# The first gate row of an FFN: by SBUF-to-SBUF transfers instead of by way of memory

## The chip, the cores and the metric

The kernel runs on one core of a Trainium2 chip. The metric is the device time of one execution in microseconds (us): the median of three runs. Engines are named as in the profile: PE (matmuls; PEld is its weight load), DVE (the vector engine), ACT (activations), POOL (GpSimd), and SP, whose queue (SPq) issues most transfers.

## What is computed

Two layers act on `x`, 32 batches of 128 tokens with 128 features, all in float32. Each layer adds an FFN of a conditioned mixture of experts to `x`:

```
x = x + L0_ffn(L0_cond(x, cond))
x = x + L1_ffn(L1_cond(x, cond))
```

The change lies in `L0_ffn`. It takes c = L0_cond(x), runs all 8 experts on every token and weights them with gates from two softmaxes:

```
router_probs = softmax(c @ w_router);  gate_weights = softmax(c @ w_gating / 0.1)
h = silu(c @ w_gate[e]) * (c @ w_up[e])          # for each expert e
expert_out[e] = h @ w_down[e]
cw = router_probs * gate_weights;  cw = cw / (sum(cw) + 1e-9)
out = sum over e of cw[e] * expert_out[e]
```

The kernel puts the gate on the input of the up projection: it multiplies c by row e of `cw` before `w_up[e]`, which is the same since silu sees only the other projection.

## The kernel before

Activations lie with features on the 128 partitions and tokens along the free axis. The 4096 tokens are cut into 8 blocks of 512 (`NB`, `TB`; 4 batches each), and a superblock is 4 blocks (`SB`). The result c of the first mixture is `c0T[blk]`, the slices of the tile `c0all`.

**Before the FFN.** Units of the first mixture run in a software pipeline, `up` of the next unit ahead of `down` of the present one. The last three are the shared expert's blocks 5, 6 and 7: `shared_up` (L297, matmuls on L302) and `shared_down` (L309, matmuls on L313); L315 on DVE adds the result into `c0T[blk]`. A table of hooks, `between` (L687), hangs the FFN's gates for blocks 0 to 3 into these last units: the router's logits, `ffn_logits(0)`, `ffn_gates(0)` (an Exp on ACT on L657, then a chain of small DVE instructions on L658 to L665 that ends in the tile `cwT`), and at the start of `shared_down(6)` `first_rows` (L683).

**The way of a gate row.** `first_rows` calls `gates_to_dram("f", 0)` (L626): a PE transpose of `cwT` (L630), a DVE copy to the SBUF tile `t`, named `fg_sb` (L632), and a 64 KB transfer to a tile in memory, `fg` (L634, SP). After the transpose, partition 16 e + b of `t` holds the gates of expert e for the 128 tokens of batch b. Then `fetch_rows(0)` (L670) issues four transfers on SP (L676), each of which brings the rows of experts k and k + 4 of one block to partition 32 k of an SBUF tile named `fgT`. One row is 512 gates, those of an expert for a block.

**The FFN.** Its 64 units are (block, expert), block by block. For each, `gate_ahead` (L747) has POOL spread a row over 128 partitions (`spread`, L707; the broadcast is L710) into one of four `bc` buffers, tile `fg`; `input_ahead` (L754) has DVE multiply it with `c0T[blk]` (L759) into the tile `cg`. `ffn_up` (L762) starts with `gate_ahead(i + 2)` and `input_ahead(i + 1)`, then takes four chunks of 128 hidden features: a gate projection from `c0T` and `wg_t`, an up projection from `cg` and `wu_t` (both L262, in column halves of 64), and `glu` (L713): Silu on ACT (L715) and a product on DVE (L716) into `hf`. `ffn_down` (L787) runs the down projection (L798) with DVE combinations of `hf` and `t` (L777 to L780). The calls for the first unit stand in this order: `gate_ahead(0)`, `gate_ahead(1)`, `input_ahead(0)`, then `ffn_up(0, 0)`.

**What orders the work.** Projections take PSUM banks from a ring of six (`mm_tile`, L118), in the order of the source; a bank is used again when ACT (gate projection) or DVE (up projection) has read it. Each engine works through its own list in order. The lists are drawn up when the kernel is built, and a matmul need not stand where the source has it unless `keep_in_program_order` pins it; L262 with halves of 64 columns is not pinned. SP issues in order too, and a transfer that waits holds up those behind it. Among them are loads for the second layer (L901), which wait for weights tiles to come free.

Of the kernel before, what the change touches and what calls it, by code (L numbers as in the profile page):

```python
# [32 lines left out]
F32 = mybir.dt.float32  # L33
# [5 lines left out]
P = 128  # L39
B, S, D = 32, 128, 128  # L40
BB = 4
TB = BB * S
# [56 lines left out]
def adaln_ffn(  # L99
# [3 lines left out]
    nc = tc.nc  # L103
# [5 lines left out]
    work = ctx.enter_context(tc.tile_pool(name="work", bufs=2))  # L109
# [8 lines left out]
    def mm_tile(name):  # L118
        taken["mm"] += 1
        return banks[:, (taken["mm"] - 1) % NM, :]  # L120
# [505 lines left out]
    def gates_to_dram(kind, sb):  # L626

        gates, name = held.pop((kind, sb)), f"{kind}g{sb}"
        ps = mm_tile(f"{name}_ps")
        nc.tensor.transpose(ps[:, :P], gates.rearrange("p e b -> p (e b)"), ident)  # L630
        t = work.tile([P, P], F32, tag="gsb", name=f"{name}_sb", bufs=1)
        V.tensor_copy(t, ps[:, :P])  # L632
        d = dram.tile([P, P], F32, tag=name, name=name)
        nc.sync.dma_start(out=d, in_=t)  # L634
        in_dram[kind, sb] = d.rearrange("(e b) t -> e (b t)", e=E1)
# [45 lines left out]
    held, in_dram, fgates = {}, {}, {}  # L681

    def first_rows():  # L683
        gates_to_dram("f", 0)
        fgates[0] = fetch_rows(0)
# [21 lines left out]
    def spread(row, name):  # L707

        bc = work.tile([P, TB], F32, tag="bc", name=name, bufs=4)
        nc.gpsimd.partition_broadcast(bc, row)  # L710
        return bc
# [33 lines left out]
    gated, bcast, sums_of = {}, {}, {}  # L745

    def gate_ahead(i):  # L747

        if i < len(ffn_units):
            blk, e = ffn_units[i]  # L750
            g, k = divmod(e, 4)
            bcast[i] = spread(fgates[blk][32 * k : 32 * k + 1, g, :], f"fg_{blk}_{e}")

    def input_ahead(i):  # L754

# [6 lines left out]
    def ffn_up(blk, e):  # L762
        i = blk * EF + e
        gate_ahead(i + 2)
        input_ahead(i + 1)
        h = work.tile([P, NC, TB], F32, tag="h", name=f"hf_{blk}_{e}", bufs=3)
        cg = gated.pop((blk, e))
        for c in range(NC):
            cs = slice(c * P, (c + 1) * P)
            g, u = mm_tile(f"g_{blk}_{e}_{c}"), mm_tile(f"u_{blk}_{e}_{c}")  # L770
            by_columns(g, wg_t[:, e, cs], c0T[blk], D // 2)
            by_columns(u, wu_t[:, e, cs], cg, D // 2)
            glu(g, u, h[:, c, :], f"sf_{blk}_{e}_{c}")
        b11, b12, b21, b22 = (h[:, k, n] for k in (slice(0, 2), slice(2, 4)) for n in (slice(0, HALF), slice(HALF, TB)))
        t = work.tile([P, 3, 2, HALF], F32, tag="bsum", name=f"t_{blk}_{e}", bufs=2)
        t2, t3, t4 = (t[:, j] for j in range(3))
        V.tensor_tensor(t3, b22, b12, ALU.subtract)  # L777
        V.tensor_tensor(b12, b12, b11, ALU.subtract)  # L778
        V.tensor_tensor(t2, b22, b12, ALU.subtract)
        V.tensor_tensor(t4, t2, b21, ALU.subtract)  # L780
        if blk == 0:
            a_prepare(e)
        if rest:
            rest.pop(0)()
        return b11, b12, b21, b22, t2, t3, t4
# [68 lines left out]
    def after_ffn(blk, e):  # L854

        if (blk, e) == (0, 2):
            logits_ahead("lg", par[:, AT["wr"]], c0T, 1)
        if (blk, e) == (0, 3):
            ffn_logits(1)
            ffn_gates(1)  # L860
        if (blk, e) == (0, 5):
            gates_to_dram("f", 1)
        if e == 4 and blk + 1 < NB:
            fgates[blk + 1] = fetch_rows(blk + 1)
        if (blk, e) == (SB, 3):
            logits_ahead("l1", par[:, AT["r1x"]], xT, 0)
        if (blk, e) == (SB, 4):
            l1_scores(0)
        if (blk, e) == (SB, 6):
            route(0)  # L870
        if (blk, e) == (SB + 1, 0):
            gates_to_dram("r", 0)
# [30 lines left out]
    x1T = xT  # L903

    gate_ahead(0)
    gate_ahead(1)
    input_ahead(0)

# [172 lines left out]
    def strip(group, j):  # L1081

        first, n, size = GROUPS[group]
        b, half = divmod(j, SB // n)
        return first + b, slice(half * size, (half + 1) * size)
# [120 lines left out]
    for j in (2, 3):  # L1206
        b, at = strip(2, j)
# [12 lines left out]
    for j, ps in enumerate(outs):  # L1220
        b, at = strip(2, j)
        t = fins[j // 2][:, at]
# [4 lines left out]
    for j in (0, 2, 1, 3):  # L1227
        b, at = strip(2, j)
# [81 lines left out]
```

## Time and profile before

| what | value |
|---|---|
| median of three runs | 964.26 us (963.98 to 965.26) |
| the profiled execution, its own time | 964.74 us |
| its span, first to last instruction | 963.0 us |
| instructions | 15674 |
| mean granted TensorE clock | 0.999 |
| PE busy | 953.2 us, 99% of the span |
| DVE busy | 594.8 us, 62% |
| ACT busy | 352.0 us, 37% |
| POOL busy | 74.9 us, 8% |
| matmuls on L262 for gate and up projections | 263.1 and 262.8 us, 1024 instructions each |
| broadcasts of gate rows, L710 on POOL | 64, mean 1142 ns |

The span is the time from the first to the last instruction of one profiled execution; its own time is 1.74 us longer. The busy times are sums over the whole span, so an engine can be busy 99% of it and still stand still for some hundred nanoseconds at one place. Waits are inferred from semaphore events, and one that ends on several of them is put down to the one that came last. In the lists of instructions in order of time, the columns are start and duration in us, engine, line, operation, what is written and read, and the number of instructions merged into the row; in brackets stands the idle time before it.

### The profile page before, as it was taken

The page shows a single profiled execution, that of the slowest core. Times are in us where ns is not written, and L with a number is a line of the kernel's source. Part 1 is how long each engine was busy: PE and PEld are TensorE (multiplying, and loading weights), DVE is VectorE, ACT ScalarE, POOL GpSimd, SP SyncE. Part 2 cuts the span into 40 slices and gives each one's busy share as a digit, 9 for nine tenths or more (in the row PEclk, how much of TensorE's full clock was granted, in tenths as well). Part 3 has the DMA queues.
Part 4 walks back from the last instruction along what each step waited for, and adds up shares of the span by engine and source line. Part 5 has one row for each costly group of instructions (what it writes and reads, how often), then busy time and mean ns, then how long its engine had stood idle before and what let it go on. Part 6 is the DMA issues. An engine that isn't in the chain of part 4 may idle for free.

```text
span 963.0 us, 15674 instructions
## 1 busy us (share of the span) xinstructions
PE 953.2 (99%) x6132; PEld 444.3 (46%) x6132; DVE 594.8 (62%) x1121; ACT 352.0 (37%) x622; POOL 74.9 (8%) x86
## 2 busy tenths in 40 slices
PE   9999999999999999999999999999999999999997
PEld 4588983444444444444444444444444443322333
DVE  4444565766866776686676786667667655633423
ACT  5354544232322322232231332223223223557674
POOL 0000002101101010110101011010110000000000
PEclk9999999999999999999999999999999999999999
DMA  9655641000000000000000000000000004040101
GB/s 331 229 156 167 209 134 49 1 1 4 1 1 2 1 1 1 1 1 1 2 2 1 1 2 3 1 2 1 1 1 1 1 1 89 2 91 1 45 1 45
DMA packets 22850, 38.13 MB, mean 40 GB/s; under 512 B 1968, under 2 KB 13232, under 8 KB 22768
## 3 DMA queue, kind: packets, MB, share of 16 engines
q1 hardware_dynamic: 22192, 36.48, 12.5%
q8 instruction: 53, 0.87, 0.4%
q10 hardware_dynamic: 576, 0.54, 0.2%
q14 instruction: 29, 0.24, 0.1%
HBM read 34.65 MB, written 2.36 MB: 38 GB/s over the span
## 4 chain that ended last, share of the span: by engine, by line
PE 83%; DVE 1%; ACT 1%; issue 0%; POOL 0%; DVEq 0%; POOLq 0%; ACTq 0%
PE banks L262 57%; PE banks L798 20%; PE banks L938 3%; PE banks L1032 1%; PE banks L313 1%; ACT hl L1040 0%; PE banks L601 0%; PE banks L302 0%; PE banks L616 0%; PE banks L546 0%; ACT L657 0%; DVE cg L759 0%; PE banks L630 0%; DVE pg L1026 0%; DVE pT L1027 0%
## 5 line engine op out<-in xcount | busy, mean ns | idle before, releaser
L715 ACT ACTIVATE sf<-banks 128x512 f32<-128x512 f32 x256 | 152.7, 597 | 433.8 <-PE banks L262 423.3
L716 DVE TENSOR_TENSOR hf<-sf,banks 128x512 f32<-128x512 f32 x256 | 175.1, 686 | 181.6 <-PE banks L262 180.5
L262 PE MATMUL banks<-c0all,wg_t 128*64 128x512 f32 x1024 | 263.1, 593 | 0.0
L262 PE MATMUL banks<-cg,wu_t 128*64 128x512 f32 x1024 | 262.8, 592 | 0.3 <-DVE cg L759 0.3
L262 PEld LDWEIGHTS banks<-cg,wu_t 128*64 128x64 f32 x1024 | 73.3, 137 | 146.9 <-issue 126.3
L262 PEld LDWEIGHTS banks<-c0all,wg_t 128*64 128x64 f32 x1024 | 72.8, 137 | 121.4 <-issue 108.8
L710 POOL PARTITION_BROADCAST fg<-fgT x64 | 72.5, 1142 | 652.7 <-DVE cg L759 492.0
L798 PE MATMUL banks<-t,wd_t 128*64 128x256 f32 x512 | 121.0, 379 | 0.0
L798 PE MATMUL banks<-hf,wd_t 128*64 128x256 f32 x512 | 104.2, 379 | 0.0
L798 PEld LDWEIGHTS banks<-hf,wd_t 128*64 128x64 f32 x512 | 53.3, 137 | 55.4 <-issue 36.8
L798 PEld LDWEIGHTS banks<-t,wd_t 128*64 128x64 f32 x512 | 70.1, 137 | 0.0
L536 ACT ACTIVATE h<-banks,w 128x256 f32<-128x256 f32 (+3 forms) x136 | 49.7, 434 | 49.4 <-PE banks L533 49.3
L798 PE MATMUL banks<-hf,a_sum 128*64 128x256 f32 x512 | 66.1, 379 | 0.0
L798 PE MATMUL banks<-t,a_sum 128*64 128x256 f32 x256 | 65.7, 379 | 0.0
L778 DVE TENSOR_TENSOR hf<-hf 128x512 f32<-128x512 f32 x64 | 63.0, 985 | 2.2
L262 PE MATMUL banks<-xall,rw_t 128*32 128x512 f32 x512 | 58.3, 593 | 0.2 <-ACT hl L1040 0.2
L262 PE MATMUL banks<-xall,sws 128*32 128x512 f32 x512 | 57.4, 593 | 0.2 <-ACT hl L1040 0.2
L546 PE MATMUL banks<-h,w 128*128 128x256 f32 (+3 forms) x272 | 52.6, 338 | 0.5 <-PEq L591 0.5
L533 PE MATMUL banks<-x,w 128*128 128x256 f32 (+3 forms) x272 | 52.2, 337 | 0.0
L533 PEld LDWEIGHTS banks<-x,w 128*128 128x128 f32 x272 | 45.3, 190 | 4.4 <-issue 1.0
L546 PEld LDWEIGHTS banks<-h,w 128*128 128x128 f32 x272 | 44.6, 190 | 5.4 <-DVE c0all L553 1.3
L1013 ACT ACTIVATE hr<-banks 128x512 f32<-128x512 f32 x64 | 36.9, 592 | 25.5 <-PE banks L262 25.4
(217 smaller groups left out, 778.3 us busy)
## 6 DMA issues: line engine op xcount, KB each, us to landing
w<-in_experts SPq DMA_DIRECT2D x36, 514.5 KB
wg_t<-in_w_gate SPq DMA_DIRECT2D x8, 256.0 KB
wu_t<-in_w_up SPq DMA_DIRECT2D x8, 256.0 KB
wd_t<-in_w_down SPq DMA_DIRECT2D x8, 256.0 KB
gates<-rg SPq DMA_DIRECT2D x4, 512.0 KB
gates<-rg SPq DMA_DIRECT2D x8, 256.0 KB
xall<-in_x SPq DMA_DIRECT2D x7, 256.0 KB
out<-fin SPq DMA_DIRECT2D x6, 256.0 KB
```

The costliest lines, as they stand in the source:

```text
L262: mm = nc.tensor.matmul(ps[own, :], lhsT=w[:, own], rhs=x, start=True, stop=True)
L313: nc.tensor.matmul(y, lhsT=sw2_t[:, c, :], rhs=h[:, c, :], start=(c == 0), stop=(c == NC - 1))
L533: nc.tensor.matmul(ps[c][:, :m, :n], lhsT=w1, rhs=x[:, :m, :n], start=True, stop=True)
L536: nc.scalar.activation(h[:, c, :m, :n], ps[c][:, :m, :n], AF.Gelu_apprx_tanh, bias=bias)
L546: nc.tensor.matmul(y[:, :m, :n], lhsT=w2, rhs=h[:, c, :m, :n], start=(c == 0), stop=(c == NC - 1))
L710: nc.gpsimd.partition_broadcast(bc, row)
L715: silu = nc.scalar.activation(s, ps_gate, AF.Silu)
L716: V.tensor_tensor(h, s, ps_up, ALU.mult)
L778: V.tensor_tensor(b12, b12, b11, ALU.subtract)
L798: nc.tensor.matmul(y[half, n], lhsT=w[:, c, :], rhs=h[:, c, :], start=first, stop=(e == EF - 1 and last))
L938: in_order(nc.tensor.matmul(y[32 * j : 32 * (j + 1)], lhsT=w, rhs=h, start=first, stop=last))
L1013: in_order(nc.scalar.activation(h[:, at, :], ps, AF.Gelu))
```

## The change

For the first superblock of the FFN's gates, `gates_to_dram` issues four transfers of 512 bytes each on SP before the transfer to memory. They take partitions 0 to 3 of `t`, which are expert 0's gates for the four batches of block 0, and lay them side by side on one partition of a new SBUF tile of 512 elements. `gate_ahead(0)` spreads that tile. The transfer to memory and the four of `fetch_rows(0)` stay as they are, and all other rows come from them.

```
--- before
+++ after
@@ -630,6 +630,11 @@
         nc.tensor.transpose(ps[:, :P], gates.rearrange("p e b -> p (e b)"), ident)
         t = work.tile([P, P], F32, tag="gsb", name=f"{name}_sb", bufs=1)
         V.tensor_copy(t, ps[:, :P])
+        if (kind, sb) == ("f", 0):
+
+            held["first row"] = work.tile([1, TB], F32, tag="first", name="first_row", bufs=1)
+            for b in range(BB):
+                nc.sync.dma_start(out=held["first row"][:, b * P : (b + 1) * P], in_=t[b : b + 1, :])
         d = dram.tile([P, P], F32, tag=name, name=name)
         nc.sync.dma_start(out=d, in_=t)
         in_dram[kind, sb] = d.rearrange("(e b) t -> e (b t)", e=E1)
@@ -749,7 +754,8 @@
         if i < len(ffn_units):
             blk, e = ffn_units[i]
             g, k = divmod(e, 4)
-            bcast[i] = spread(fgates[blk][32 * k : 32 * k + 1, g, :], f"fg_{blk}_{e}")
+            row = held["first row"] if i == 0 else fgates[blk][32 * k : 32 * k + 1, g, :]
+            bcast[i] = spread(row, f"fg_{blk}_{e}")
```

More of the change, by code (lines that the diff above doesn't have):

```diff
@@ L632, in gates_to_dram @@
         V.tensor_copy(t, ps[:, :P])
+        if (kind, sb) == ("f", 0):
+            held["first row"] = work.tile([1, TB], F32, tag="first", name="first_row", bufs=1)
+            for b in range(BB):
+                nc.sync.dma_start(out=held["first row"][:, b * P : (b + 1) * P], in_=t[b : b + 1, :])
         d = dram.tile([P, P], F32, tag=name, name=name)
@@ L751, in gate_ahead @@
             g, k = divmod(e, 4)
-            bcast[i] = spread(fgates[blk][32 * k : 32 * k + 1, g, :], f"fg_{blk}_{e}")
+            row = held["first row"] if i == 0 else fgates[blk][32 * k : 32 * k + 1, g, :]
+            bcast[i] = spread(row, f"fg_{blk}_{e}")
     def input_ahead(i):
```

## The prediction

> **What bounds the kernel now.** I read the page first. PE is busy 953.2 of 963.0 us at a granted clock of 0.999:
>
> ```profile
> span 963.0 us, 15674 instructions
> PE 953.2 (99%) x6132; PEld 444.3 (46%) x6132; DVE 594.8 (62%) x1121; ACT 352.0 (37%) x622; POOL 74.9 (8%) x86
> ```
>
> So the change can only win what PE stands still because of the first gate row. Next, the chain of waits around the FFN's start (start, length in us, what):
>
> ```profile
> 158.33 4.31 PE banks L313 x10
> 162.64 0.02 issue
> 162.66 0.76 DVE c0all L315
> 163.42 0.01 issue
> 163.43 0.04 POOLq L710
> 163.47 0.13 issue
> 163.60 0.81 POOL fg L710
> 164.41 0.02 issue
> 164.43 1.16 DVE cg L759
> 165.58 0.04 issue
> 165.63 11.38 PE banks L262 x52
> ```
>
> The row does sit on this chain: POOL's broadcast, DVE's product, then PE. The list of instructions in order of time on PE tells how long PE really stands:
>
> ```profile
> 162.55 2.79 PE L262 MATMUL banks<-c0all,wg_t 128*64 128x512 f32 x12
> 165.63 2.79 PE L262 MATMUL banks<-cg,wu_t 128*64 128x512 f32 x12 [0.28 <-DVE cg L759]
> 168.25 1.03 PE L262 MATMUL banks<-c0all,wg_t 128*64 128x512 f32 x4
> 169.11 1.03 PE L262 MATMUL banks<-cg,wu_t 128*64 128x512 f32 x4
> 169.97 1.03 PE L262 MATMUL banks<-c0all,wg_t 128*64 128x512 f32 x4
> ```
>
> The source has gate and up projections in turns; the built order is three gate projections, then three up projections, so PE has work that needs no gate. Groups of four (one projection) start 0.86 us apart (168.25, 169.11, 169.97), and three after a pause take 2.62 (165.63 to 168.25). Three gate projections from 162.55 therefore end their turn at 165.17. PE goes on at 165.63. **The stall is 0.46 us**, 0.05% of the kernel; the 0.28 in the row is smaller because it runs from the modelled end. Last, SP's queue and its waits:
>
> ```profile
> 158.68 0.34 SPq L634 DMA_DIRECT2D fg<-fg_sb  x1
> 161.50 2.47 SPq L676 DMA_DIRECT2D fgT<-fg  x4
> 164.08 0.39 SPq L901 DMA_DIRECT2D sws<-in_s_w  x1
> ```
>
> ```profile
> SPq L676 <- DMA fg<-fg_sb: 2.4, 1, 2.4
> ```
>
> The row goes out at 158.68, is in memory at 161.48, is read back from 161.50 and lands at 163.40 by the trace's semaphore records: 4.72 us. The chain names L315 (end 163.41) as what released POOL, 0.01 us after that landing. POOL's next two broadcasts follow the landings of their rows by the same 0.02 us, so I take the transfer as the cause.
>
> **First row.** Four transfers of 512 bytes are added. The nearest row for their issue is L676, also to one partition: starts at 161.50, 162.26, 162.86 and 163.44, so 0.75 and then 0.6 apart. The fourth goes out at 158.68 + 0.75 + 0.6 + 0.58 = 160.61. No SBUF-to-SBUF transfer is in the trace. Above, I bound the landing by the reads of L676, 1.78 to 1.93 us from issue; below, by what is known of its halves: L634, which reads SBUF, has its first packet 0.84 us after issue, and L676, which writes SBUF, lands 0.4 us after its packets: 1.25. The fourth lands at 161.9 to 162.5; I take 162.5, since L676 is the whole path. That is 0.9 us earlier than 163.40.
>
> The Trainium skill speaks against this: "DMA: Bandwidth & Descriptors", in "Rules for kernel authors", wants many small transfers merged into one, for under 64 KB nearly all is overhead, and "Anatomy of one DMA" gives a fixed cost of about 2.0 us each (fitted on the GpSimd path). Four in a row at that price land at 166.7, the first product is ready at about 168.6, and PE would stand 3 us longer than now. The rows say that the fixed parts overlap: four reads take 1.78 + 1.94 = 3.7 us in all, not 8. The rows decide.
>
> POOL now waits for four transfers instead of one; its wait instruction takes 0.04 us, so 0.13 more. Broadcast from 162.5 + 0.2 + 0.13 = 162.8 to 163.6 (0.80 each). DVE's product stands behind L315, which ends at 163.41, so it starts at 163.65. It took 1.145 us beside POOL's second broadcast, 0.68 elsewhere; it ends between 164.35 and 164.8. PE wants it at 165.17: the margin is 0.4 to 0.8 us, and **the whole 0.46 goes**. The other 0.3 to 0.8 us of the gain lie beside PE's three gate projections and are worth nothing.
>
> **What the four issues push back.** Everything behind them on SP starts 0.75 + 0.6 + 0.58 + 0.58 = 2.5 us later: the 64 KB write from 158.68 to 161.20, the four of L676, one load of L901, and block 1's four rows. The last two aren't needed for tens of microseconds (block 1 starts eight units of 9.9 us later). L901 waits for the end of L313 at 162.6; should it come ahead of L676, it adds 0.5 us to the rows.
>
> The second row matters. The write took 2.80 us here, but 1.54 to 1.57 us at its three other places (232, 581 and 847 us): in this one instance one of 16 engines began its packets at 160.42, when a 16 KB instruction fetch (159.30 to 160.43) had ended. Issued at 161.20 it should miss that fetch: in memory at 162.76. Then the second read goes out 0.77 later and lands 1.93 after that, at 165.46 (164.19 before). Broadcast 165.65 to 166.45, product on DVE, beside the third broadcast, 166.47 to 167.6.
>
> Who waits behind it? If DVE's list stays as it is, `cg` of unit 1 stands ahead of the first L716. In the rows before, the two products run from 164.43 to 166.64 and the first L716 starts at 166.82 and ends at 167.51. Now it runs from 167.68 to 168.37. The fourth up projection needs the PSUM bank that it frees. PE comes there at 165.17 + 2.57 + 0.86 = 168.60, and its weight load, which carries the wait, has to start some 0.2 us before: 168.4. So the new wait is just covered, with 0.03 us to spare, and I count 0 to 0.2 for it. ACT and POOL behind them have slack (ACT idles 1.1 us and more before each later L715).
>
> Here a second rule bears: "SBUF — State Buffer", "Who interferes with whom", says that a two-input DVE instruction and a GpSimd one hold a shared port for their whole length, the other fully blocked. If the third broadcast (0.8) came first, the product would end at 0.68 + 0.8 after its start, 167.95, and PE would stall 0.35. The row for just this pairing has 1.145, so I keep that.
>
> **Sum.** -0.46 for the stall, +0.1 for the second row, 0 for everything behind PE: -0.36 us. On the profiled execution 964.74 (span 963.0 and 1.74 around it) that makes 964.38; the median of the runs lies 0.48 below it, 964.26, and gives 963.9. About 0.2%, 1.9 us, is what a measurement of this kernel can tell from no change: I forecast no change.
>
> **Rivals.**
>
> *Slower, by the second row.* One mechanism: the write in memory is late again (the fetch moves along with the program, or the write meets it anyway), so row 1 comes late, and DVE, in order, holds the first L716 and with it PE's fourth up projection. With 2.80 us for the write L716 ends at 169.6, the stall is 1.2 us, and the kernel is 0.75 us slower: 965.0. For: the order on DVE before, and the thin margin. Against: three clean writes. It loses from the point where the write takes over 2.0 us; for 0.2% it would have to take 4, which no row shows.
>
> *Another order of the matmuls.* The row is expected earlier, so the up projections could be built in source order, or L716 ahead of the second product. With the first up projection right behind the first gate projection, PE asks for `cg` at 163.45 and gets it at 164.4 to 164.8: stall 0.9 to 1.3, 0.5 to 0.9 us slower, 965.0. With L716 first, the gain is a clean 0.46: 963.8. An order that changes along all 64 units could cost some us; units there repeat every 9.89 us, which is just the sum of their matmuls (16 groups of 0.43 and 14 of 0.217), so none can be gained.
>
> *Nothing.* The four transfers take as long as the way by memory, or POOL does wait for L315: the first broadcast starts at 163.6 as before, 964.3.
>
> **Chances.** The forecast (stall gone, second row nearly covered) 0.55, 963.8 to 964.2; second row late 0.18; another order 0.17, of it half beyond 0.2%; nothing 0.10. Beyond 0.2% lie half of the case of another order (0.085, slower 0.06: an order that hurts over many units; faster 0.025: one that is better at a place I can't point to) and 0.09 of the others together (slower 0.05: a write and a row later than any seen; faster 0.04). So faster 0.065, within 0.2% 0.825, slower 0.11. Range: below 964.26 - 0.5 for the whole gain and 0.5 for the scatter of runs (963.98 to 965.26); above 0.9 for the rivals and 0.6 of scatter: 963.2 to 965.8.
>
> **What would show it.** Right: the first broadcast starts at 162.4 to 162.9, the fourth new transfer at about 160.6, and PE passes from the gate to the up projections without a pause. Second step: L634 at 161.2, second broadcast at 165.6, first L716 ending near 168.4, the load of the fourth up projection waiting at most 0.2 us on it. Wrong: a first broadcast after 163.6 (transfers in series), up projections in another place in PE's list, or a change of over 2 us in units far from the FFN's start.

## The result, and the profile after

The changed kernel takes 965.84 us in the median of 22 runs (965.09 to 966.61), the kernel before 964.39 in 22 runs beside them (963.97 to 965.66). The ratio is 1.0014 with a 95% interval of 1.0008 to 1.0020: slower by 1.45 us. That is within the 0.2% which I gave the best chance, but with the other sign than the forecast's -0.36 us, and 0.04 us above the top of the range that I gave.

The page of the changed kernel, to be held against the first lines shown of before:

```profile
span 964.5 us, 15682 instructions
PE 954.1 (99%) x6132; PEld 446.6 (46%) x6132; DVE 593.5 (62%) x1121; ACT 352.1 (37%) x622; POOL 74.5 (8%) x86
```

PE has the same 6132 matmuls and is busy 0.9 us longer; the profiled execution's own time is 966.22 us. The chain of waits around the FFN's start (start, length, what):

```profile
162.69 0.03 issue
162.72 0.76 DVE c0all L315
163.48 0.09 issue
163.56 0.80 POOL fg L715
164.37 0.02 issue
164.39 0.70 DVE cg L765
165.09 0.04 issue
165.14 12.24 PE banks L262 x56
```

(L715 and L765 are L710 and L759 of before, moved by the new lines.) POOL's first broadcast starts at 163.56, where it was 163.60: the new way of the row is hardly shorter. The product takes 0.70 instead of 1.16, since no second broadcast runs beside it. PE starts the up projections 0.5 us earlier than before, and yet loses. The list in order of time on PE shows why:

```profile
162.61 1.93 PE L262 MATMUL banks<-c0all,wg_t 128*64 128x512 f32 x6
165.14 1.50 PE L262 MATMUL banks<-cg,wu_t 128*64 128x512 f32 x5 [0.60 <-DVE cg L765]
166.05 0.59 PE L262 MATMUL banks<-c0all,wg_t 128*64 128x512 f32 x1
166.48 0.59 PE L262 MATMUL banks<-cg,wu_t 128*64 128x512 f32 x1
166.48 1.01 PE L262 MATMUL banks<-c0all,wg_t 128*64 128x512 f32 x2
166.91 0.59 PE L262 MATMUL banks<-cg,wu_t 128*64 128x512 f32 x1
```

A projection is four instructions, two passes for each half of the columns; the two halves of a projection run side by side. Before, PE had 12 gate instructions, then 12 up. Now it has 6, one projection and a half, and from then on gate and up rows are mixed. The built lists say it exactly; here are their first entries, shortened and counted in halves of the columns:

```
before:  L262 c0all,wg_t x6 | cg,wu_t x6 | c0all,wg_t x2 | cg,wu_t x2 ...
after:   L262 c0all,wg_t x3 | cg,wu_t x2 | c0all,wg_t    | cg,wu_t x2 | c0all,wg_t x2 | cg,wu_t x2 ...
```

The third half, the lower one of the second gate projection, is followed by another lower half. In the trace its two passes start at 163.52 and 163.95 with nothing beside them, while the passes of a lower and an upper half that are neighbours start in pairs within 0.01 us. A narrower view shows the half by itself:

```profile
163.52 1.02 PE L262 MATMUL banks<-c0all,wg_t 128*64 128x512 f32 x2
```

Two instructions take the time here in which a whole projection has four (1.03 in the rows of before). The list is changed by the build, not by the diff; why it drew up this one is not shown. SP's queue:

```profile
158.74 3.53 SPq L637 DMA_DIRECT2D first_row<-fg_sb  x4
162.32 0.58 SPq L639 DMA_DIRECT2D fg<-fg_sb  x1
163.00 0.38 SPq L907 DMA_DIRECT2D sws<-in_s_w  x1
```

The four issues take 3.53 us, not 2.5; one row gives the reason in part (minimum, median and longest of the four, in ns):

```profile
L637 SPq DMA_DIRECT2D first_row<-fg_sb x4: 588/606/1600, 158.7 to 161.7; - x4
```

### The profile page after: what moved, and what is told of

Same layout as the page of the kernel before. It is cut to its first block, busy times and chain, and to the rows that moved or that the text cites. A ratio compares the mean times of both kernels' runs of the same rounds, so it can differ in the third digit from the quotient of the medians.

```text
span 964.5 us, 15682 instructions
## 1 busy us (share of the span) xinstructions
PE 954.1 (99%) x6132; PEld 446.6 (46%) x6132; DVE 593.5 (62%) x1121; ACT 352.1 (37%) x622; POOL 74.5 (8%) x86
## 4 chain that ended last, share of the span: by engine, by line
PE 83%; ACT 1%; DVE 1%; issue 0%; POOL 0%; DVEq 0%; ACTq 0%
PE banks L262 57%; PE banks L804 20%; PE banks L944 3%; PE banks L1038 1%; PE banks L313 1%; ACT hl L1046 0%; PE banks L601 0%; PE banks L302 0%; PE banks L616 0%; PE banks L546 0%; ACT L662 0%; PE banks L630 0%; DVE pg L1032 0%; DVE pT L1033 0%; PE banks L276 0%
## 5 line engine op out<-in xcount | busy, mean ns | idle before, releaser
L721 DVE TENSOR_TENSOR hf<-sf,banks 128x512 f32<-128x512 f32 x256 | 174.9, 686 | 184.0 <-PE banks L262 183.4
L262 PE MATMUL banks<-cg,wu_t 128*64 128x512 f32 x1024 | 273.6, 592 | 0.6 <-DVE cg L765 0.6
L262 PE MATMUL banks<-c0all,wg_t 128*64 128x512 f32 x1024 | 274.0, 593 | 0.0
L262 PEld LDWEIGHTS banks<-cg,wu_t 128*64 128x64 f32 x1024 | 77.0, 137 | 146.3 <-issue 125.5
L262 PEld LDWEIGHTS banks<-c0all,wg_t 128*64 128x64 f32 x1024 | 76.3, 137 | 121.3 <-issue 108.7
L715 POOL PARTITION_BROADCAST fg<-fgT x63 | 71.4, 1139 | 493.6 <-DVE cg L765 491.2
L804 PE MATMUL banks<-hf,a_sum 128*64 128x256 f32 x512 | 68.5, 379 | 0.0
L262 PE MATMUL banks<-xall,rw_t 128*32 128x512 f32 x512 | 58.3, 593 | 0.2 <-ACT hl L1046 0.2
L262 PE MATMUL banks<-xall,sws 128*32 128x512 f32 x512 | 57.4, 593 | 0.2 <-ACT hl L1046 0.2
```

The costliest lines, as they stand in the source:

```text
L262: mm = nc.tensor.matmul(ps[own, :], lhsT=w[:, own], rhs=x, start=True, stop=True)
L721: V.tensor_tensor(h, s, ps_up, ALU.mult)
L804: nc.tensor.matmul(y[half, n], lhsT=w[:, c, :], rhs=h[:, c, :], start=first, stop=(e == EF - 1 and last))
```

## The experiments

My theory after the trace: the loss is made by PE's new list, 0.86 us for the half that stands alone (two passes of 0.43) and 0.32 for asking for the product one and a half projections early, against a stall before; and 0.25 more arise behind the last transfer. The rival: the transfers in SP's queue and the rows that come late behind them.

The start of the FFN moves by up to 1.4 us from profile to profile (first gate projection at 161.66 to 163.06; matmuls at 40 us are shifted as much), so each trace is measured from its own first gate projection. The columns: PE's pause between the first gate and the first up projections (from a regular next start, 0.43 after the last, to the actual one); from the first gate projection to unit 2's first Silu, less the 18.38 us of before; from the landing of the last output to the kernel's end; and the median beside before in the same session.

| kernel | pause | Silu of unit 2 | end | median, and before | ratio, interval |
|---|---|---|---|---|---|
| before | 0.44 | 0 | 1.00 | | |
| changed | 0.76 | +1.16 | 1.25 | 965.84, 964.39 | 1.0014, 1.0008 to 1.0020 |
| pin_after | 0 | -0.50 | 1.25 | 964.35, 964.61 | 0.9996, 0.9987 to 1.0004 |
| order_before | 1.02 | +1.42 | 1.00 | 966.72, 964.61 | 1.0020, 1.0011 to 1.0029 |
| spare4_before | 0.31 | -0.13 | 1.25 | 964.88, 964.61 | 1.0001, 0.9993 to 1.0009 |
| gates4_before | 0 | -0.50 | 1.00 | 964.17, 964.61 | 0.9995, 0.9987 to 1.0004 |
| gates4_again | 0 | -0.50 | 1.00 | 963.80, 964.63 | 0.9994, 0.9985 to 1.0002 |
| pairs_after | 0.41 | -0.03 | 1.25 | 964.71, 964.63 | 1.0002, 0.9994 to 1.0011 |
| queue_only | 0.83 | +0.45 | 1.25 | 965.43, 964.63 | 1.0010, 1.0003 to 1.0016 |
| transfers_later | 1.68 | +2.14 | 1.25 | one run, 967.35 | |
| spare8_end | | | 1.00 | one run, 964.06 | |

The third column follows from the second: without a pause it is -0.50; a pause adds itself and 0.05 for the new start; a half alone adds 0.86. For the changed kernel -0.50 + 0.76 + 0.05 + 0.86 = 1.17. From that Silu to the FFN's end the traces run alike: 200 Silus after the first, the changed kernel is still 1.18 behind.

**pin_after.** The changed kernel, unit 0's matmuls pinned to their old order (the edit is shortened here):

```
+        if i == 0:
+            for kind, c, half in [...]:      # g0 g1 g2 u0 u1 u2 g3 u3, each lower half, then upper
+                ...
+                tc.keep_in_program_order(nc.tensor.matmul(...))
+                ...
```

> The changed kernel with unit 0's projections pinned to the order that they had before (three gate projections, three up, the fourth of each). Main theory (the loss is PE's new order: one column half alone costs 0.86 us, and asking for the product earlier costs 0.31; 0.25 more lies behind the last transfer): no half alone, the product is ready at about 165.1 and wanted at 165.2, so no stall; 0.45 won, 0.25 still lost at the end: 0.2 us below before, PE's end 0.4 earlier. Rival (the transfers in SP's queue and the late second row cost the time): still 1.2 to 1.5 us above before.

PE's list in order of time (its L782 is unit 0's L262):

```profile
163.06 2.79 PE L782 MATMUL banks<-c0all,wg_t 128*64 128x512 f32 x12
165.69 2.74 PE L782 MATMUL banks<-cg,wu_t 128*64 128x512 f32 x12
168.26 1.03 PE L782 MATMUL banks<-c0all,wg_t 128*64 128x512 f32 x4
```

The up projections start 2.63 us after the gate projections, with no pause: 0.50 won at the FFN's start, 0.25 lost at the end. The median lies 0.26 below before, as expected, though the interval takes in no change. With all its transfers in place the kernel is not slower: but for the 0.25 at the end, the transfers aren't the loss.

**order_before.** The kernel before, no new transfers, unit 0 pinned to the changed kernel's list (`g0`, lower `g1`, `u0`, upper `g1`, `u1`, then in turns).

> The kernel before, without the new transfers, with unit 0's projections pinned to the order of the changed kernel (a gate projection, the lower half of the second, an up projection, the upper half, then in turns). Main theory: 0.86 us for the half alone, and PE asks for the product at 164.3 and gets it at 165.6, a stall of 1.3 where it was 0.45: 1.7 us above before. Rival (transfers): same as before within 0.2 us.

```profile
161.66 1.93 PE L776 MATMUL banks<-c0all,wg_t 128*64 128x512 f32 x6
164.44 1.50 PE L776 MATMUL banks<-cg,wu_t 128*64 128x512 f32 x5 [0.85 <-DVE cg L759]
165.36 0.59 PE L776 MATMUL banks<-c0all,wg_t 128*64 128x512 f32 x1
```

The order alone costs 1.42 in the trace and 2.1 in the medians, interval 1.1 to 2.8 us (the profiled execution, at 965.26, is the fastest of the twelve). The pause is 1.02 instead of the 1.3 that I expected, since the row came 0.2 us earlier in this profile. The rival's "same" is excluded.

**pairs_after.** As pin_after, with `g0 g1 u0 u1 g2 u2 g3 u3`: PE asks nearly as early as in the changed kernel, but in whole projections.

> The changed kernel with unit 0 pinned to two gate projections, then two up projections, then in turns: PE asks for the product where the changed kernel does (after two gate projections), but no column half stands alone. Main theory: 0.86 us below the changed kernel; against before, 0.3 for the earlier question, 0.25 at the end, 0.55 above. Rival (not the half alone but the early question, or the transfers, makes the loss): as the changed kernel, 1.4 above before.

```profile
162.24 1.94 PE L782 MATMUL banks<-c0all,wg_t 128*64 128x512 f32 x8
164.43 1.94 PE L782 MATMUL banks<-cg,wu_t 128*64 128x512 f32 x8 [0.25 <-DVE cg L765]
```

The half alone is gone, and 1.19 us with it in the trace, 0.86 by the half and 0.35 by a shorter pause (0.41; the row came 0.34 us earlier here, as the second transfer was held less, 1.25 us). It is at 0.08 above before in the median, the interval from -0.6 to +1.1, where 0.55 was expected: consistent, and the changed kernel's 1.45 lies outside.

**queue_only.** As pin_after, but the first broadcast reads the old row, so the transfers only stand in the way.

> The changed kernel with the four transfers issued, but the first broadcast reading the row that comes by way of memory; unit 0 pinned as in pin_after. Main theory (the write and the reads behind the four transfers start 2.7 us later): the first row lands at about 166.1, the broadcast runs from 166.3, the product is ready at 167.8 to 168.3. PE's list now has two of unit 1's gate projections ahead of the first up projection, so it asks at 166.95: a stall of 0.9 to 1.3 where it was 0.45, and 0.25 at the end: 0.7 to 1.1 above before. Rival (what is behind the transfers is hidden): 0.25 above.

The first broadcast starts 3.33 us after the first gate projection (1.05 before). The build put two of unit 1's gate projections ahead of the first up projection, which covers 1.7 of it. A pause of 0.83 is left: 0.45 later at unit 2, 0.25 at the end, 0.8 in the medians. So what SP does behind four transfers is a real price, 2.3 us of delay for a row; the changed kernel escapes it, since no other row was wanted so early.

**spare4_before and spare8_end.** The kernel before with unread transfers from one SBUF tile to another; the build put them at 60 us, among the loads, not in the FFN where the source has them. The comment in the edit is added here; spare8_end has eight transfers of 256 bytes, since a tile for eight of 512 does not fit in SBUF beside the others.

```
+        if (blk, e) == (2, 0):
+            spare = work.tile([1, TB], F32, tag="first", name="spare", bufs=1)
+            for j in range(BB):          # spare8_end: range(8), 64 columns each
+                nc.sync.dma_start(out=spare[:, j * P : (j + 1) * P], in_=ident[j : j + 1, :])
```

> The kernel before, with four transfers of 512 bytes between SBUF tiles added in the middle of the FFN, whose result nobody reads. Theory of the end (the transfers' semaphores are handed out in turn, eight of them; four more transfers shift which one the last output transfer carries, and SP checks them one after the other): 0.25 us above before, all of it between the landing of the last output and SP's last wait. Rival (the 0.24 us at the end is scatter): same as before. Also the price of such a transfer undisturbed: main theory issue 0.6 us each and landing 1.65 us after issue, on 16 engines in 32-byte pieces.

> As spare4_before, but eight unread transfers of 256 bytes instead of four of 512, so that the eight semaphores come round to where they were. Theory of the end: from the landing of the last output to the end 1.00 us, as before, not 1.25. Rival (every added transfer lengthens the end): 1.5.

In the traces, 0.25 appears with four transfers and is gone with eight. The eight transfer semaphores are handed out in turn, and at the end SP goes through them in seven checks in a fixed order (the first check takes two of them), one each 0.06 us. Before, the last output carries the sixth of the eight, and two checks follow it; shifted by four it carries the second, six follow, and 4 x 0.0625 = 0.25. The column of the end in the table agrees in every trace: 1.25 where four transfers are added, 1.00 where none or eight are. The medians can't show it (0.27 above, interval -0.7 to +0.9). In the same profile the price of an undisturbed transfer was not to be had: among the loads the four took over 2 us to land.

**gates4_before, gates4_again.** The kernel before, no transfers, all four gate projections of unit 0 ahead of its up projections, banks taken in that order.

> The kernel before, no transfers added, with unit 0's four gate projections pinned ahead of its four up projections (the banks taken in that order). Main theory: the fourth gate projection, 0.86 us, covers the stall of 0.45 at the first gate row, so PE never waits for it: 0.45 us below before, and below the changed kernel by 1.9. Rival (something else than PE's wait bounds the FFN's start, such as DVE's list): no gain.

> The kernel gates4_before once more, since its gain lay inside its interval: 0.45 us below before in the median, and in the trace no pause of PE between the gate and up projections of unit 0.

The second profile's list on PE:

```profile
162.97 3.65 PE L775 MATMUL banks<-c0all,wg_t 128*64 128x512 f32 x16
166.46 3.60 PE L775 MATMUL banks<-cg,wu_t 128*64 128x512 f32 x16
169.89 1.03 PE L262 MATMUL banks<-c0all,wg_t 128*64 128x512 f32 x4
```

No pause (3.49 us for four projections, 0.05 of it the new start), and 0.50 us less in both traces. The medians lie 0.44 and 0.83 below before; both intervals reach just above 1. Taken as independent, the two together give 0.63 below with an estimated interval of 0.06 to 1.2, so the time alone barely proves it. These are the lowest medians of all versions in the same sessions, and there is no new transfer.

**transfers_later.** As pin_after, with DVE copying the four rows eight times over first, so that the transfers are issued after the instruction fetch.

> As pin_after, but the transfers read a copy of the gates' first four partitions that DVE makes eight times over, some 1.5 us later, so that they are issued when the 16 KB instruction fetch that starts 0.6 us after the gates' copy is over; SP's list has the write to memory ahead of them. Theory of the fetch (the second transfer was held on SP for 1.2 to 1.6 us because one of the 16 engines that each of them uses was busy with the fetch): issues of 0.6 us throughout, the fourth landing 1.65 us after its issue, at about 164. Rival (a second such transfer is held in any case): the second again takes over 1.2 us. The time says little, as the row comes later.

```profile
158.88 0.34 SPq L642 DMA_DIRECT2D fg<-fg_sb  x1
162.17 0.71 SPq L684 DMA_DIRECT2D fgT<-fg  x1
162.98 2.46 SPq L640 DMA_DIRECT2D first_row<-again  x4
```

The four issues now take 0.57 to 0.59 us each, 2.46 in all with their gaps, and each lands 1.68 to 1.72 us after its issue. The second isn't held. This favours the fetch, though I moved the transfers and not the fetch, and their place in SP's list changed too. The four traces that have the transfers at the old place say the same: the fetch takes 1.29 us in the changed kernel, 0.93 in pin_after and pairs_after, 1.04 in queue_only, the second issue takes 1.60, 1.24, 1.25 and 1.34, and it ends 0.37 to 0.38 us after the fetch in all of them. The kernel's time is that of a late row, and of another half alone: the build put three of unit 1's gate halves ahead (-0.50 + 1.68 + 0.05 + 0.86 = 2.09, measured 2.14).

## Why the prediction was wrong, step by step

- **What bounds the kernel: right.** PE, and a stall of 0.46 that could be won: 0.44 in the records, and 0.50 with the new start. Both gates4 runs and pin_after win just that.
- **"The built order is three gate projections, then three up projections": the step that failed.** I read it from the trace of before and carried it into the sum as if it were fixed. I had the other order as a rival at 0.17, and its pause of 0.9 to 1.3 was of the right kind (0.76). But I priced it only as a pause; that a list broken in the middle of a projection leaves half of PE's columns idle for 0.86 us was nowhere in the sum. The stall of 0.46 did not go but grew to 0.76, and with the 0.86 this order costs 1.18 of the measured 1.45: order_before has the loss without the transfers, and pin_after and pairs_after have the transfers without the loss.
- **Behind PE 0: wrong by 0.25.** I counted SP's later issues as harmless and never asked which semaphore the kernel's end would wait for last. spare4_before and spare8_end show it.
- **The sum as measured:** 0.76 - 0.44 + 0.86 + 0.25 = 1.43; the medians differ by 1.45. That the two agree to 0.02 is luck in part: the pause in kernels with the list of before is 0.31 to 0.44 from profile to profile.
- **"About 0.2% is what a measurement can tell from no change": too coarse.** With 22 runs on each side the interval is 0.6 us to either side, and 1.45 us is clear of it.
- **The first row, landing at 162.5: too early by 0.9.** Undisturbed, the price was right: issues 0.6 apart, landing in 1.7 us, between my bounds of 1.25 and 1.93. But I sent one write past the 16 KB fetch and forgot that the new transfers stand in the write's old place. In every trace the fetch starts about 0.6 us after SP's first issue there. Each 512-byte transfer runs as 16 pieces of 32 bytes, so it too can have a piece behind the fetch: of the first, one piece starts at 160.63, as the fetch ends, and completes at 161.73, 1.27 us after the other 15, and the second holds SP for 1.60. The 0.13 for a wait on four transfers did not appear: the broadcast follows the last landing by 0.19, as it did before. With pin_after the row came soon enough even so.
- **The rival "POOL does wait for L315": excluded.** The first broadcast starts at 163.56 almost as before, and the chain names L315 again. But in pin_after it starts while L315 still runs, to 163.92, and 0.19 after the landing at 163.48:

```profile
163.17 0.75 DVE L315 SCALAR_TENSOR_TENSOR c0all<-banks,par,c0all 128x512 f32<-128x512 f32 x1 [2.68 <-PE banks L313]
163.67 0.79 POOL L715 PARTITION_BROADCAST fg<-first_row  x1 [160.75 <-DMA first_row<-fg_sb]
```

- **The product at 0.68 us when no broadcast runs beside it: right,** 0.69. It is why PE got its product earlier at all.
- **The write behind the four transfers, 1.54 to 1.57: near,** about 1.8 (162.32 to the first read at 164.11), clear of the fetch.
- **The second row holding the first L716: did not happen.** DVE's list changed as well: three products of L721 now stand ahead of unit 1's L765. The mechanism of my slower rival thus had no place, while the lateness that it was built on was real: the second broadcast starts at 166.83, 2.4 us later than before, counted from the first gate projection.
- **The two rules that I weighed:** small transfers overlapped in their fixed parts, as the rows said: the fourth landed 4.63 us after the first issue, the fetch's hold included, where four in series came to 8. The product beside the second broadcast takes 1.03 to 1.15 us in the traces that have the two together, neither 0.68 nor 0.68 with the whole 0.80 added; the changed kernel has no such pair.

## What to carry to other kernels

Where a build draws up the engines' lists, a changed dependence can move matmuls that the diff does not touch: compare the built lists before counting a gain, and pin those whose pairing matters. The stall on a late operand was cheaper to cover here with work of the same engine (four gate projections first) than to shorten by new transfers, which delay all that stands behind them in their queue. A gain of half a microsecond has to be followed in the trace; the medians of a dozen runs barely see it.

## What the runs showed of the hardware that I had not expected

A column half of 64 that has no partner of the other half next to it in PE's list costs its full two passes, 0.86 us. A transfer of 512 bytes, which runs in 16 pieces, was as exposed as one of 64 KB to a 16 KB instruction fetch, which took 0.93 to 1.57 us here: one piece of the first was late by 1.27 us, and the second held SP until 0.37 us after the fetch. And four more transfers moved the kernel's end by 0.25 us, eight by nothing.
